# Second-to-last block through the short residual path, a bias addition split by tiles and issued at another place, and two projections exchanged at the end of the first layer

## The chip, the cores and the metric

The kernel runs on one core of a Trainium2 chip. The time is that of one execution on the device, in microseconds (us). Before the change three runs gave 1673.42, 1675.89 and 1676.69 us; the median is 1675.89 us. Lower is better.

## What is computed

Four sub-layers follow each other on 4 x 1024 tokens of 256 numbers each. Every one is `x = x + layernorm(f(layernorm(x)))`:

```python
x = x + _layernorm(_L0_attn_ref(_layernorm(x), ...))   # gated attention in groups of 64
x = x + _layernorm(_L0_ffn_ref(_layernorm(x), ...))    # low-rank feed-forward, 256-64-1024-64-256
x = x + _layernorm(_L1_attn_ref(_layernorm(x), ...))   # 16 heads, relu scores divided by their sum
x = x + _layernorm(_L1_ffn_ref(_layernorm(x), ...))    # 8 experts, each takes its top tokens
...
def _L1_attn_ref(x, w_qkv, w_out, b_out, gamma, beta):
    ...
    out = out @ w_out + b_out
    y = x + out
    ...
```

The change is in the first two sub-layers (the "first layer") and in the hand-over to the third. `b_out` is the output's bias that the title speaks of; in the kernel it is added to the normalised input `h` ahead of time, because `h` is what `out @ w_out` is later added to.

## The kernel before

**Tiling.** The 4096 tokens are 8 blocks of 512 (`NB = 8`), each held as four tiles of 128 tokens (`NJ = 4`) by 256 numbers. A batch row is two blocks (`BPB = 2`). The residual stream `xs[0]` to `xs[7]` stays in SBUF from start to end.

**Engines.** TensorE (PE) does all matrix products and transposes. VectorE (DVE) and ScalarE (ACT) empty PSUM, make statistics and scale. GpSimd (POOL) has a few element-wise additions and the power -1/2 of each layer norm. PE, DVE and ACT execute in the order in which the kernel is written (`manual_schedule` names just these three). POOL is not among them: the tool that builds the program places POOL's instructions itself.

**The first layer** is one pipeline over the blocks. In iteration `t` of the loop, the attention of block t, the projections of block t+1, and the feed-forward of block t-1 (in part t-2) are woven together step by step on PE (`woven`, `attend`, `project`, `feed_forward`). In iteration 7 there is no block 8, and the projections of the second layer's first row stand in its place: `project_row` with steps `turn` (transpose `h`), `queries`, `keys`, `values`, for `k = 0` and `k = 1` (blocks 0 and 1).

**Side work on DVE and ACT** is written as chains (`Chain`, `start`): lists of pairs of a gap and a step. `on_pe` issues one PE step, advances a clock of planned time by the step's length, and then issues those chain steps that are due. A larger gap therefore puts a step later in the order of DVE and ACT, behind the work that other steps issue there.

**The usual path** from attention to the feed-forward of a block is `add_normalized("c", t, y)`: four statistics of `y` (`stc`, `mvc`), `vec`, the power on POOL (`rsc`, L539), `msc` (L543), four scalings of `y` on ACT (L549), one addition `x += y` of 128x1024 on POOL (L560). Then come four statistics of `x` (`stf`, `mvf`), `vef`, `rsf` on POOL, `msf`, four scalings `f` on DVE (L807), and the PE transpose of `f` (`turn` in `feed_forward`, L818) with which the feed-forward begins.

**The short path**, `ahead` in `feed_forward`, is in use for block 7 alone: the statistics of each tile of `y` are made as soon as the tile is there (`then` in `attend`); ACT subtracts the mean from `x` in four pieces (`shift_x`, L909), and DVE adds `y * rs` to `x` tile by tile (L915) and makes the statistics of that tile at once. POOL's 128x1024 addition falls away.

**The bias** `b1o` (from `b_out`) is added by POOL to all of `h` after the second `turn` of a block (L339), one instruction of 128x1024; it must stand behind the transposes, which need `h` without it. `h` is read again only when the second layer closes that block (L1128).

**The end of the first layer** (the loop over `*left[:2], ..., second["values1"], keys0, keys0`) is PE work of the last feed-forwards and of the second row's projections. The last three steps are `values1` of block 1 and then `keys0` of blocks 0 and 1. `keys` empties its PSUM through ACT (L357) and then DVE (L358) into `kT`; the scores of the second layer (L1217) need `kT`.

The gaps concerned are these:

```python
POW, ADD = 4.0, 4.0
SOON = 2.0
gap = POW if t < NB - 2 else SOON                                            # add_normalized, L562
gap, add_gap = (POW, ADD) if t < NB - 2 else (SOON, ADD - 1.0)               # feed_forward, usual path, L900
gap = SOON                                                                   # feed_forward, short path, L918
```

Of the kernel before, what the change touches and what calls it, by code (L numbers as in the profile page):

```python
# [13 lines left out]
ALU = mybir.AluOpType  # L14
# [4 lines left out]
P = 128  # L19
D = 256  # L20
DC = D // P
TB = 512
NJ = TB // P
# [48 lines left out]
def kernel(  # L72
# [32 lines left out]
    nc = tc.nc  # L105
    B, S, _ = x_in.shape
    NT = B * S
    NB = NT // TB
    NTILE = NT // P
    BPB = S // TB  # L110
# [109 lines left out]
    with ExitStack() as st1:  # L220
# [101 lines left out]
            row["v"] = act_v("vaug")  # L322
            return row

        def row_steps(row, k, bank, new_hT):

            h = row["h"][k]
            cols = slice(k * TB, (k + 1) * TB)
            d = {}

            def turn(c):
                if c == 0:
                    d["hT"] = new_hT()
                tp = bank([P, NJ, P], "tp")
                for i in range(NJ):
                    nc.tensor.transpose(tp[:, i, :], h[:, i, c * P : (c + 1) * P], ident)
                nc.scalar.copy(d["hT"][c], tp.rearrange("p j t -> p (j t)"))
                if c == DC - 1:
                    nc.gpsimd.tensor_tensor(h, h, b1o.unsqueeze(1).to_broadcast([P, NJ, D]), ALU.add)  # L339

            def rows_of(w, t, name):
                pp = bank([P, TB], name)
                for c in range(DC):
                    nc.tensor.matmul(  # L344
                        pp, lhsT=w[:, c, t * P : (t + 1) * P], rhs=d["hT"][c], start=(c == 0), stop=(c == DC - 1)
                    )
                return pp

            def queries(t):
                nc.scalar.copy(row["qT"][:, t, cols], rows_of(wq1, t, "pq"))  # L350

            def keys(t):
                if t not in row["kT"]:
                    row["kT"][t] = act8("hid", "kT").rearrange("p (r a) n -> p r (a n)", r=2)
                kT = row["kT"][t]
                pk = rows_of(wk1, t, "pk")
                nc.scalar.activation(kT[:, 0, cols], pk, AF.Copy, scale=strip[:, 0:1])  # L357
                nc.vector.tensor_scalar(kT[:, 1, cols], pk, strip[:, 1:2], None, ALU.mult)  # L358

            def values(z):  # L360
                v = row["v"]
                if (k, z) == (0, 0):
                    nc.gpsimd.memset(v[:, :, :, HD : HD + 1], 1.0)
                pv = bank([P, 2, D], "pv")
                for y in range(2):
                    i = 2 * z + y
                    for c in range(DC):
                        nc.tensor.matmul(  # L368
                            pv[:, y, :],
                            lhsT=d["hT"][c][:, i * P : (i + 1) * P],  # L370
                            rhs=wv[:, c, :],
                            start=(c == 0),
                            stop=(c == DC - 1),
                        )
                j = k * NJ + 2 * z
                nc.scalar.copy(
                    v[:, j : j + 2, :, 0:HD].rearrange("p j h d -> p (j h) d"),
                    pv.rearrange("p j (h d) -> p (j h) d", d=HD),
                )

            return {"turn": turn, "queries": queries, "keys": keys, "values": values}
# [124 lines left out]
        def start(*steps):  # L506
            chains.append(Chain(steps))
            return chains[-1]
# [10 lines left out]
                time["spent"] += 1.0  # L519

        POW, ADD = 4.0, 4.0
        SOON = 2.0

        def stats_steps(tag, src):

# [27 lines left out]
        def add_normalized(tag, t, y):  # L553

            r, stats, scales, shift = stats_steps(tag, y)

            def apply(i0):
                apply_on_act(y(), y(), r, i0)
                if i0:
                    nc.gpsimd.tensor_tensor(xs[t], xs[t], y(), ALU.add)  # L560

            gap = POW if t < NB - 2 else SOON  # L562
            return [*stats, (0.0, scales), (gap, shift), (0.5, lambda: apply(0)), (0.0, lambda: apply(2))]

        def open_block(t):
# [165 lines left out]

        def project_row(row, k, new_hT, chain):

            steps = row_steps(row, k, bank, new_hT)

            def turn(z):
                chain.finish()
                steps["turn"](z)

            named = {f"turn{z}": (0.6, lambda z=z: turn(z)) for z in range(2)}  # L740
            for name in ("queries", "keys", "values"):
                for z in range(2):
                    named[f"{name}{z}"] = (1.75, lambda name=name, z=z: steps[name](z))
            return named
# [53 lines left out]
        def feed_forward(t, y, ahead=None):  # L798

            d = {}  # L800
# [96 lines left out]
                start(*add_normalized("g", t, lambda: d["y"]))  # L897

            if ahead is None:
                gap, add_gap = (POW, ADD) if t < NB - 2 else (SOON, ADD - 1.0)  # L900
                adding = [*add_normalized("c", t, y), (add_gap, stats[0][1]), *stats[1:]]
            else:

                ra, scales_a, shift_a = ahead

                def shift_x():
                    shift_a()
                    for i in range(NJ):
                        nc.scalar.activation(  # L909
                            xs[t][:, i, :], xs[t][:, i, :], AF.Identity, bias=ra["ms"][:, i : i + 1]  # L910
                        )

                def add(i):
                    x = xs[t][:, i, :]
                    nc.vector.scalar_tensor_tensor(x, y()[:, i, :], ra["rs"][:, i : i + 1], x, ALU.mult, ALU.add)  # L915
                    stats[i][1]()

                gap = SOON  # L918
                adding = [(0.0, scales_a), (gap, shift_x), *((0.0, lambda i=i: add(i)) for i in range(NJ))]
# [30 lines left out]
        for t in range(NB):  # L950
            opening.finish()
            coming, after = after, None
            to_hidden, hidden, from_hidden = ffn
            adding = ahead = then = None
            if t == 0:
                whole = later_counts()
            elif t == 1:
                mb1, strip, same_b, earlier_b, bits, counts, fold = later_constants(whole)
                count_p, count_c, count_t, in_tile = (
                    whole[name] for name in ("count_p", "count_c", "count_t", "in_tile")  # L960
                )
            if coming is not None:
                own = project(coming)
                adding = start(*residual(coming))
            else:

                row0 = open_row(hs)
                inputs = opening, start(*normalize_row(hs[1], 1))
                of_row = [project_row(row0, k, new, inputs[k]) for k, new in enumerate((first_hT, second_hT))]
                own = [  # L970
                    of_row[0][name]
                    for name in ("turn0", "turn1", "queries0", "queries1", "keys1", "values0", "values1")
                ]
                d["y"] = wk.tile([P, NJ, D], F32, tag="nT", name="y", bufs=1)
                ra, stats, scales_a, shift_a = stats_steps("c", lambda d=d: d["y"])
                ahead, then = (ra, scales_a, shift_a), lambda i, stats=stats: stats[i][1]()
            if t + 2 < NB:
                after, steps = open_block(t + 2)
                opening = start(*steps)
            elif coming is not None:  # L980

                d["y"] = act4("y")
                hs = [act4("h") for _ in range(BPB)]
                opening = start(*normalize_row(hs[0], 0))
            beside = woven(left, own, to_hidden)
            main = attend(d, then)
            while main:
                on_pe(*main.pop(0))
                if not beside and hidden:
                    on_pe(*hidden.pop(0))  # L990
                places = max(len(main) - len(hidden), 0) + 1
                for _ in range(-(-len(beside) // places)):
                    on_pe(*beside.pop(0))
            for step in (*beside, *hidden):
                on_pe(*step)
            if adding is not None:
                adding.finish()
            left = from_hidden
            ffn = feed_forward(t, lambda d=d: d["y"], ahead)
            chains.insert(0, chains.pop())  # L1000
            d = coming
# [3 lines left out]
        for step in (  # L1005
# [6 lines left out]
            *to_hidden[2:],  # L1012
            *hidden,
            *from_hidden,
            second["values1"],
            *(of_row[k]["keys0"] for k in range(BPB)),
        ):
            on_pe(*step)
        for chain in chains:
# [7 lines left out]
    with ExitStack() as st3:  # L1027
# [243 lines left out]
                    rest[:0] = divide(state, t)  # L1271

        row = row0
        before = None
        for b in range(B):
            after = open_row() if b + 1 < B else None
# [397 lines left out]
```

## Time and profile before

| what | us |
| --- | --- |
| median of three runs (lowest, highest) | 1675.89 (1673.42, 1676.69) |
| the profiled execution, its own time | 1674.0 |
| its span, first to last instruction | 1671.5 |
| PE busy in the span | 1548.5 (93%) |
| DVE, ACT, POOL busy | 914.9, 634.6, 388.1 |
| first layer, from the start to about | 428 |
| PE busy in the stretch 310 to 432 | 111.3 of 122 |
| PE busy in the second layer's attention, 432 to 1090 | 653.0 of 658 |

The profile is of one execution. Its times run from the first instruction, and 2.5 us of the execution's 1674.0 us lie outside of the span. A line of the timeline gives the start and the length in us, the engine, the source line, the operation, the tiles written and read, the shape, and how many instructions are merged in it; in brackets stands how long the engine sat idle before, and what released it. PE matmuls of float32 appear as two records each.

### The profile page before, as it was taken

How to read it: one execution, taken by the hardware profiler on the slowest of the kernel's cores; microseconds unless marked ns; L12 is line 12 of the kernel's file. 1: busy time of each engine (PE TensorE's matmuls, PEld its weight loads, DVE VectorE, ACT ScalarE, POOL GpSimd, SP SyncE). 2: the span in 40 equal slices, each digit the busy share in tenths (PEclk: the TensorE clock that was granted, in tenths of full speed). 3: DMA queues.
4: the chain of work that ended last, by engine and by line, in shares of the span. 5: the costliest groups of instructions: out<-in, count | busy, mean ns of one | idle time of the engine just before them, and what ended most of it. 6: DMA issues, size and time to landing. Idle time of an engine off the chain costs nothing.

```text
span 1671.5 us, 22249 instructions
## 1 busy us (share of the span) xinstructions
PE 1548.5 (93%) x8663; PEld 770.4 (46%) x8663; DVE 914.9 (55%) x2046; ACT 634.6 (38%) x1099; POOL 388.1 (23%) x396
## 2 busy tenths in 40 slices
PE   7999999998999999999999999924999999999990
PEld 3666666665222232323222222202765766667670
DVE  4555556654657787878787888775121122212115
ACT  3344444534444545454545455421212122121213
POOL 4122233222201010201011101012332432433325
PEclk9999999999999999999999999955999999999995
DMA  8300000000000000000000000041233333423217
GB/s 210 107 1 1 1 1 1 1 1 1 1 1 1 14 14 13 15 13 14 14 14 1 13 5 10 8 147 26 63 66 76 68 67 71 93 46 84 32 19 208
DMA packets 66195, 64.31 MB, mean 38 GB/s; under 512 B 23181, under 2 KB 60074, under 8 KB 65962
## 3 DMA queue, kind: packets, MB, share of 16 engines
q1 hardware_dynamic: 52352, 42.81, 8.5%
q0 software_dynamic: 12864, 19.14, 6.9%
q8 instruction: 68, 1.11, 0.3%
q10 hardware_dynamic: 874, 0.93, 0.2%
q14 instruction: 37, 0.30, 0.1%
HBM read 39.64 MB, written 23.23 MB: 38 GB/s over the span
## 4 chain that ended last, share of the span: by engine, by line
PE 91%; DVE 3%; issue 3%; POOL 1%; DMA 1%; ACT 1%; SPq 0%; POOLq 0%; ACTq 0%; DVEq 0%
PE sc L1217 16%; PE po L1233 15%; PE py L1548 13%; PE ph L1526 13%; PE pg L679 3%; PE py L787 3%; PE pv L695 3%; PE pv L368 2%; PE ph L843 2%; PE po L759 2%; PE pt L1121 2%; PE pk L344 2%; PE pq L344 2%; PE pq L864 2%; PE po L763 1%
## 5 line engine op out<-in xcount | busy, mean ns | idle before, releaser
L1227 DVE TENSOR_SCALAR w<-sc 128x1024 f32<-128x1024 f32 x256 | 312.6, 1222 | 97.1 <-PE sc L1217 64.1
L1226 ACT ACTIVATE w<-sc 128x512 f32<-128x512 f32 x512 | 278.0, 594 | 229.1 <-PE sc L1217 102.5
L1217 PE MATMUL sc<-qT,kT 32*128 32x512 f32 x2048 | 293.6, 639 | 2.3 <-DVE kT L358 1.6
L1233 PE MATMUL po<-w,vaug 128*17 128x512 f32 x2048 | 274.7, 598 | 0.9 <-DVE w L1227 0.2
L1548 PE MATMUL py<-w,hid 128*128 128x256 f32 x1024 | 230.1, 380 | 0.0
L1533 ACT ACTIVATE hid<-ph,mb 128x512 f32<-128x512 f32 (+1 forms) x136 | 90.1, 662 | 365.4 <-PE ph L1526 365.4
L1526 PE MATMUL ph<-xT,w 128*128 128x512 f32 (+1 forms) x544 | 224.7, 572 | 0.5 <-DVE xT L1510 0.4
L1548 PEld LDWEIGHTS py<-w,hid 128*128 128x128 f32 x1024 | 191.1, 190 | 32.0 <-issue 7.5
L1217 PEld LDWEIGHTS sc<-qT,kT 32*128 32x128 f32 x2048 | 80.8, 183 | 186.1 <-issue 170.7
L1526 PEld LDWEIGHTS ph<-xT,w 128*128 128x128 f32 x544 | 104.6, 193 | 111.6 <-issue 107.6
L1562 POOL DMA_INDIRECT acc_d<-y,idx x64 | 101.3, 1582 | 211.5 <-issue 150.7
L1233 PEld LDWEIGHTS po<-w,vaug 128*17 128x17 f32 x2048 | 35.3, 95 | 200.0 <-issue 171.0
L1560 DVE TENSOR_TENSOR y<-py,mb 128x256 f32<-128x256 f32 x64 | 26.8, 418 | 183.9 <-PE py L1548 183.9
L1485 POOL DMA_INDIRECT got<-tok_d,idx x64 | 66.0, 1031 | 152.9 <-DVE idx L1481 135.8
L1510 DVE COPY xT<-tp 128x512 f32<-128x512 f32 (+1 forms) x34 | 22.4, 660 | 97.4 <-PE tp L1508 97.4
L1053 POOL TENSOR_TENSOR rsg<-veg,mhalf 128x1 f32<-128x1 f32 x32 | 17.8, 555 | 219.2 <-DVE veg L1052 219.2
L679 PE MATMUL pg<-nT,wh 128*128 128x512 f32 x128 | 61.6, 613 | 1.5 <-ACT nT L618 1.5
L787 PE MATMUL py<-wo,oT 128*128 128x256 f32 x256 | 61.9, 385 | 0.0
L695 PE MATMUL pv<-wh,nT 128*128 128x512 f32 x128 | 59.7, 593 | 0.0
L1481 DVE CAST idx<-parts 128x8 int32<-128x8 f32 x8 | 1.3, 167 | 101.9 <-PE parts L1479 101.9
L787 PEld LDWEIGHTS py<-wo,oT 128*128 128x128 f32 x256 | 47.3, 190 | 17.2 <-issue 9.4
L560 POOL TENSOR_TENSOR x<-x,y 128x1024 f32<-128x1024 f32 x15 | 35.3, 2353 | 75.7 <-ACT y L549 75.7
(262 smaller groups left out, 1855.0 us busy)
## 6 DMA issues: line engine op xcount, KB each, us to landing
w<-in_L_ffn_W_dram SPq DMA_DIRECT2D x16, 1024.0 KB, 5.7
x<-in_L_attn_x_dram SPq DMA_DIRECT2D x8, 512.0 KB, 5.0
acc_d<-logits SPq DMA_DIRECT2D x8, 512.0 KB, 5.1
tok_d<-hg SPq DMA_DIRECT2D x32, 128.0 KB, 1.8
back<-acc_d SPq DMA_DIRECT2D x7, 512.0 KB, 9.2
out_dram<-x SPq DMA_DIRECT2D x16, 128.0 KB, 1.7
out_dram<-back POOLq DMA_DIRECT2D x4, 512.0 KB, 6.7
out_dram<-x SPq DMA_DIRECT2D x3, 512.0 KB, 3.4
```

The costliest lines, as they stand in the source:

```text
L344: nc.tensor.matmul(pp, lhsT=w[:, c, t * P : (t + 1) * P], rhs=d["hT"][c], start=(c == 0), stop=(c == DC - 1))
L679: nc.tensor.matmul(pg, lhsT=wh[:, c, HID + e * P : HID + (e + 1) * P], rhs=d["nT"][:, c, :], start=(c == 0), stop=(c == DC - 1),)
L695: nc.tensor.matmul(pv, lhsT=d["nT"][:, c, i * P : (i + 1) * P], rhs=wh[:, c, 0:HID], start=(c == 0), stop=(c == DC - 1),)
L787: nc.tensor.matmul(py, lhsT=d["oT"][:, e, :], rhs=wo[:, e, :], start=(e == 0), stop=(e == EC - 1))
L1217: nc.tensor.matmul(sc, lhsT=row["kT"][t][rows, r, kt * P : (kt + 1) * P], rhs=row["qT"][rows, t, qh * TB : (qh + 1) * TB], start=True, sto ...
L1226: nc.scalar.activation(w[:, j, :], sc, AF.Relu)
L1227: nc.vector.tensor_scalar(w[:, 2:4, :], pair, 0.0, None, ALU.max)
L1233: nc.tensor.matmul(po[32 * j : 32 * j + HD + 1, :], lhsT=row["v"][:, kt, HQ * t + 2 * j + r, :], rhs=w[:, j, :], start=(kt == 0), stop=(kt ...
L1526: nc.tensor.matmul(ph, lhsT=w1[:, c, f * P : (f + 1) * P], rhs=xT[u][:, c, h * n : (h + 1) * n], start=(c == 0), stop=(c == DC - 1),)
L1533: nc.scalar.activation(hid[:, f, h * n : (h + 1) * n], ph, AF.Gelu, bias=mb1[:, e * FC + f : e * FC + f + 1])
L1548: nc.tensor.matmul(py, lhsT=hid[:, f, i * P : (i + 1) * P], rhs=w2[:, f, :], start=(f == 0), stop=(f == FC - 1),)
L1562: scatter = nc.gpsimd.indirect_dma_start(out=acc_d[:, :], out_offset=bass.IndirectOffsetOnAxis(ap=lists[e].idx[:, k : k + 1], axis=0), in_ ...
```

## The change

Five edits:

- Block 6, the second to last, takes the short path too. The lines that set `ahead` and `then` move from the branch of iteration 7 to a place that iterations 6 and 7 both reach.
- The gaps: `SOON` becomes 1.0. With that the short path of both blocks plans 1.0 behind each power. In `add_normalized` the gap is 4.0 for all blocks but the last, which keeps 2.0; so block 6's second normalisation (tag "g", after its feed-forward) goes from 2.0 to 4.0.
- The bias is added by four instructions of 128x256 in place of one of 128x1024, in both layers (`add_bias`).
- For the first row (`row0`, blocks 0 and 1) the bias is not added in `turn` but by two calls of `add_bias` at the start of the second layer's main loop.
- At the end of the first layer both `keys0` come ahead of `values1`.

```diff
+        def add_bias(row, k):
+
+            for i in range(NJ):
+                nc.gpsimd.tensor_tensor(row["h"][k][:, i, :], row["h"][k][:, i, :], b1o, ALU.add)
+
-        def row_steps(row, k, bank, new_hT):
+        def row_steps(row, k, bank, new_hT, with_bias=True):
...
-                if c == DC - 1:
-                    nc.gpsimd.tensor_tensor(h, h, b1o.unsqueeze(1).to_broadcast([P, NJ, D]), ALU.add)
+                if c == DC - 1 and with_bias:
+                    add_bias(row, k)
...
-        SOON = 2.0
+        SOON = 1.0
...
-            gap = POW if t < NB - 2 else SOON
+            gap = POW if t < NB - 1 else 2.0
...
-            steps = row_steps(row, k, bank, new_hT)
+            steps = row_steps(row, k, bank, new_hT, False)
...
-                gap, add_gap = (POW, ADD) if t < NB - 2 else (SOON, ADD - 1.0)
-                adding = [*add_normalized("c", t, y), (add_gap, stats[0][1]), *stats[1:]]
+                gap = POW
+                adding = [*add_normalized("c", t, y), (ADD, stats[0][1]), *stats[1:]]
...
-                ra, stats, scales_a, shift_a = stats_steps("c", lambda d=d: d["y"])
-                ahead, then = (ra, scales_a, shift_a), lambda i, stats=stats: stats[i][1]()
...
+            if t >= NB - 2:
+                ra, stats, scales_a, shift_a = stats_steps("c", lambda d=d: d["y"])
+                ahead, then = (ra, scales_a, shift_a), lambda i, stats=stats: stats[i][1]()
...
-            second["values1"],
             *(of_row[k]["keys0"] for k in range(BPB)),
+            second["values1"],
...
         row = row0
+        for k in range(BPB):
+            add_bias(row, k)
```

## The prediction

> **What bounds the kernel now.** I read the page, PE's waits up to 432 us, and then the timeline of the end of the first layer engine by engine. The page gives the bound:
>
> ```profile
> span 1671.5 us, 22249 instructions
> ...
> PE 1548.5 (93%) x8663; PEld 770.4 (46%) x8663; DVE 914.9 (55%) x2046; ACT 634.6 (38%) x1099; POOL 388.1 (23%) x396
> ...
> PE 91%; DVE 3%; issue 3%; POOL 1%; DMA 1%; ACT 1%; SPq 0%; POOLq 0%; ACTq 0%; DVEq 0%
> ```
>
> PE is the chain. Faster side work gains only where PE waits for it. PE's waits between 362 and 432 us (waiting line, releaser: total, times, longest):
>
> ```profile
> PE tp L818 <- DVE f L807: 6.5, 2, 3.3
> PE sc L1217 <- DVE kT L358: 1.6, 1, 1.6
> PE sc L1217 <- ACT w L1226: 0.7, 1, 0.7
> ```
>
> In the second layer's main part PE is busy 653.0 of 658 us: nothing to win there, something to lose. PE's timeline places the waits:
>
> ```profile
> 361.54 1.88 PE L344 MATMUL pk<-hT,wk 128*128 128x512 f32 x4
> ...
> 367.42 1.36 PE L818 MATMUL tp<-ident,f 128*128 128x128 f32 x4 [3.15 <-DVE f L807]
> 368.57 3.21 PE L368 MATMUL pv<-wv,hT 128*128 128x256 f32 x8
> ...
> 375.57 1.89 PE L368 MATMUL pv<-wv,hT 128*128 128x256 f32 x8
> ...
> 404.04 1.83 PE L818 MATMUL tp<-ident,f 128*128 128x128 f32 x8 [3.33 <-DVE f L807]
> 405.67 3.43 PE L368 MATMUL pv<-wv,hT 128*128 128x256 f32 x8
> ...
> 428.10 1.98 PE L1217 MATMUL sc<-qT,kT 32*128 32x512 f32 x10 [1.56 <-DVE kT L358]
> 430.81 1.14 PE L1217 MATMUL sc<-qT,kT 32*128 32x512 f32 x6 [0.74 <-ACT w L1226]
> ```
>
> Wait A (3.15 us) is for block 6's `f`, wait B (3.33) for block 7's. The eight `pv` matmuls behind each take 3.05 and 3.36 us from start to next start, those at 375.57 only 1.73. The windows (PE, PEld, DVE, ACT, POOL busy; then PE's clock) say why:
>
> ```profile
> 367.40:371.60 4.20, 4.18 (x12) 3.18 (x13) 1.86 (x7) 0.59 (x1) 0.00 (x0) 0.59 0.00 0
> 371.60:375.60 4.00, 4.00 (x30) 3.73 (x29) 1.92 (x7) 1.17 (x2) 0.00 (x0) 1.00 0.00 0
> ...
> 404.00:409.00 5.00, 4.96 (x16) 3.52 (x16) 2.04 (x8) 1.16 (x2) 1.01 (x1) 0.66 0.01 3
> ```
>
> After each wait the clock is down. So the waits cost more than their length. POOL and DVE inside them:
>
> ```profile
> 353.57 2.36 POOL L339 TENSOR_TENSOR h<-h,b1o 128x1024 f32<-128x1024 f32 x1 [1.38 <-PE tp L336]
> ...
> 393.93 2.36 POOL L339 TENSOR_TENSOR h<-h,b1o 128x1024 f32<-128x1024 f32 x1 [3.33 <-PE tp L336]
> ```
>
> ```profile
> 353.60 2.35 DVE L543 SCALAR_TENSOR_TENSOR msc<-mvc,rsc 128x4 f32<-128x4 f32 x1
> ...
> 394.47 2.10 DVE L915 SCALAR_TENSOR_TENSOR x<-y,rsc,x 128x256 f32<-128x256 f32 x1 [1.11 <-ACT x L909]
> ...
> 397.17 0.45 DVE L915 SCALAR_TENSOR_TENSOR x<-y,rsc,x 128x256 f32<-128x256 f32 x1
> ```
>
> The same `x` addition takes 0.45 us alone and 2.10 us while POOL adds the bias; a 128x4 `msc` (0.15 elsewhere) takes 2.35.
>
> **What the Trainium skill says.** "TensorE: Matmul & The Clock Gate", What's actually happening: about 3.4 us of idling halves PE's clock, about 3.4 us of work restores it. The trace agrees roughly: 0.59 and 0.66 follow waits of 3.15 and 3.33 us, while after the 1.56 us wait at 428 the clock stays 1.00. "SBUF — State Buffer", Who interferes with whom: a DVE instruction with two SBUF inputs and a GpSimd one that reads SBUF exclude each other for a whole instruction, and the one that issues first goes first. The 2.10 above agrees. "GPSIMD Engine Reference", 3.1 Elementwise: an addition costs 2.6 cycles of 1.2 GHz per element, 2.22 us for 1024; the trace has 2.36.
>
> **Part 1: block 6 by the short path (wait A).** The changed program's order leaves PE's alone but for the end. DVE's and ACT's change.
> Before: `y`'s last tile is written at 345.4; the four `stc` stand behind `oT` at 348.67; `vec` 350.92; `rsc` to 352.19; `msc` held to 355.95 by the bias; ACT scales to 358.05; POOL adds to 360.49; `stf` to 363.2; then DVE sits behind a `kT` until 364.84; `rsf` 365.08 to 366.18; `f` 366.87; PE 367.42.
> After: one `stc` per tile beside the attention (0.55 us each, where DVE waits 1.5 to 2.7 us for PE); `vec` behind the same `oT`, 348.7; `rsc` 1.02 us to 350.0; `msc` 350.2; ACT, idle there, shifts (4 in 1.70) to 352.0; DVE adds from 350.75. One L915 with its statistics takes 1.05 (the spacing 397.17 to 398.21); four of them, `qT` 0.34 and `kv` 0.6 end at 355.9, with two or three waits for the split bias at about 357; `vef`, `rsf` 1.2; `f` in two halves around the two `y2` writes (1.25), done at 361. PE comes for it at 364.27, 3 us later. `kT` now stands behind `f`. So wait A goes whole: 3.15. Its cold clock goes too: `tp` plus `pv` took 4.20 us (367.42 to 371.62), warm 0.43 (the four at 326.70) + 1.73 = 2.16; 2.04. **A: -5.2.** Next late would be the PSUM bank of the second `pq` (359.82 on PE): the first `y2` write now ends at about 359.7, where it ended at 358.0. Up to 0.5 could come back.
>
> **Part 2: the bias and block 7 (wait B).** In the changed program's order POOL has the four additions exactly where the one was: behind `rsc`, ahead of `rsf`, for both blocks. POOL's order isn't the kernel's, so "later" does not come about. They still start when the transposes end, beside block 7's L915. What changes is the length: by the page's price 256 elements are an estimated 0.55 us, plus 0.14 that the long one has over its price: 0.7. From both sides: an L915 waits for nothing, or for all four (2.8). I take one tile at most each time: at 218.68 to 221.5 DVE and POOL passed the port to and fro, two DVE `head` in 1.58 and two POOL ones in 1.99, neither waiting for both.
> On the clock of before: `msc` still sits behind `qT` (393.3); ACT now shifts ahead of both `hT`, so x tile 0 is ready at 393.9, not 394.35; L915 waits to 394.2 for tile 0 of the bias; four rounds of 1.05 plus some 0.6 of further waits: 398.9; `y2` writes 1.2; `vef`, `rsf` 1.3; `f` 401.6 (before 403.49; a `kT` of 0.65 in that stretch moves behind `f`); PE 402.1, before 404.04. PE itself comes later by 0.4, as `hT` 0 waits behind the shifts (its first `pq` at 395.65 for 394.84; `hT` 1 is where it was). Wait B thus shrinks from 3.33 to about 1.0, and its end by 2.1 (bounds: 0.2 if all four tiles win, 2.9 without any waiting). At 1 us no cold clock: `tp` and `pv` took 4.99, warm 2.60, of which 0.5 is PE running behind the four `f` anyway; 1.9. **B: -4.0** (0 to -4.8).
>
> **Part 3: gaps and keys first (end).** Block 6's second scaling moves on ACT behind all eight `hid`: the last `hid` no longer waits 1.96 us, `pq` (L864) takes 3.6 for 4.09: -0.45. But it ends at 418.95, POOL's `x` addition at 421.35, and the `y2` buffer that block 7 writes is free only then: 0.6 later than PE delivers (420.67). From there `y2` to `msg` (statistics, power) ends at 427.0, with ACT's `vaug` before it done at 426.65. `keys0` first makes `kT` ready at 426.4 under `values1`, and the scores start at 426.75, not 428.10, now waiting for `vaug`'s copy. Still they run only two groups: the third PSUM buffer needs the first ACT `w`, which stands behind the four L549 (2.07): 427.1 + 2.07 + 0.6 = 429.75, before 430.81. **End: -1.05** (0 if the buffer wait is longer, -2.3 if neither wait stays).
>
> **Part 4: bias tiles in the second layer.** Six rows, four tiles for one: 2.8 for 2.37 us of POOL, nothing on PE as long as DVE isn't waiting for the `rsb` behind it. Cost 0.
>
> **Sum.** 5.2 + 4.0 + 1.05 = 10.2 us, on the profiled 1674.0: 1663.8. The median of before is 1.9 above that execution; against it 1665.7. The parts' bounds give 4.7 to 12.3, so 1663.6 to 1671.2, and single runs of before spread over 3.3.
>
> **Rivals.**
> - *The port stays shut.* The four tiles follow each other without a gap, block 7's first L915 waits for all, B keeps 2.8 us and the cold clock. For: POOL's queue is full at that moment, DVE's is not. Against: 218.68. -5.2, -0.4, -1.05: 1669.2.
> - *The wait moves.* DVE, loaded with four L915 and `stf` between 350 and 357, frees PSUM banks late, and PE stops at `pq` or `po` in place of `tp`. For: the `pq` margin of 0.1. Against: `po`'s is 0.5 and the next ones over 1. It would have to eat 7 us of A and B: about 1673.
> - *Slower.* In the second layer `rsb` stands behind the bias on POOL, DVE waits in order for `rsb`, `w` (L1227) behind it, and PE two groups later. If a tile costs 1.1 us (a 128x4 power takes 1.02) the bias is 4.4, 2.0 longer, in each of six rows. It decides from 10.2 / 6 = 1.7 us a row. At 2.0, with nothing of it hidden, it is +12 - 10.2: 1677.7. Against: PE waits nowhere in those rows now though a bias of 2.37 already stands there.
>
> **How the numbers follow.** Forecast 0.67, port 0.17, moved wait 0.09, slower 0.07. The likeliest: 1665.7. The range 1661.5 to 1671.5 is the parts' bounds with the runs' spread on the low side; it holds the port too. What a measurement can tell from no change is 0.2%, 3.4 us, so faster is below 1672.5: 0.67 + 0.17 + a third of the moved wait = 0.87; same 0.06; slower 0.07.
>
> **What would show it.** A: no PE idle before L818 near 364, clock 1.00 behind it. B: the wait near 397 (5.2 earlier) of 0.5 to 1.5 us, no cold `pv`, and POOL's four 128x256 of about 0.7 with L915 of at most 1.1. End: scores released by `vaug`, a second wait on `w`. Wrong if B is over 2.5 us with a clock of 0.66, if PE waits in the second layer behind a bias, or if the bias is found elsewhere on POOL.

## The result and the profile after

Four runs of the changed kernel take 1663.58 us in the median (1663.14 to 1663.88); the kernel before takes 1676.29 beside them (four runs). The ratio is 0.9928, with a 95% interval of 0.9910 to 0.9945. The profiled executions are 10.45 us apart: 1674.0 before, 1663.55 after. In the changed file a line stands 5 to 8 further down; L823 is the old L818, L812 the old L807, L920 the old L915, L349 the old L344, L554 the old L549, L1223 the old L1217, L1232 the old L1226. The bias is L328. The kernels of e1 and e10 to e12 have line numbers of their own. Matmuls at a lowered clock are called cold here, at the full clock warm.

The page of the changed kernel, the same three lines as before:

```profile
span 1661.6 us, 22279 instructions
...
PE 1544.9 (93%) x8663; PEld 769.6 (46%) x8663; DVE 913.8 (55%) x2050; ACT 634.0 (38%) x1099; POOL 390.5 (23%) x419
...
PE 90%; issue 3%; DVE 3%; POOL 2%; DMA 1%; ACT 1%; SPq 0%; POOLq 0%; ACTq 0%; DVEq 0%
```

POOL has 23 more instructions and 2.4 us more work, PE the same number of matmuls and 3.6 us less busy time, most of it because matmuls that ran cold at the end of the first layer no longer do. PE's waits in the last part of the first layer (waiting line, releaser: total, times, longest):

```profile
PE tp L823 <- DVE f L812: 0.9, 1, 0.9
PE sc L1223 <- ACT w L1232: 0.8, 1, 0.8
PE pq L349 <- ACT hT L342: 0.7, 1, 0.7
PE sc L1223 <- ACT vaug L381: 0.7, 1, 0.7
...
```

The lines left out are three waits of 0.5 to 0.6 at `ph` and `py`, which the kernel before has too. The 6.5 us for `f` are down to 0.9, and the wait for `kT` is gone. PE's timeline at the three places:

```profile
362.69 0.60 PE L823 MATMUL tp<-ident,f 128*128 128x128 f32 x4
363.13 1.89 PE L373 MATMUL pv<-wv,hT 128*128 128x256 f32 x8
...
395.19 1.64 PE L823 MATMUL tp<-ident,f 128*128 128x128 f32 x8 [0.91 <-DVE f L812]
396.67 1.89 PE L373 MATMUL pv<-wv,hT 128*128 128x256 f32 x8
...
416.25 1.98 PE L1223 MATMUL sc<-qT,kT 32*128 32x512 f32 x10 [0.67 <-ACT vaug L381]
419.01 1.13 PE L1223 MATMUL sc<-qT,kT 32*128 32x512 f32 x6 [0.78 <-ACT w L1232]
```

At block 6's `tp` there is no bracket any more, and both `pv` groups take 1.89 us where they took 3.21 and 3.43. The windows behind both places (PE, PEld, DVE, ACT, POOL busy; then PE's clock) have the clock at 1.00, where it was 0.59 and 0.66:

```profile
362.69:366.59 3.90, 3.90 (x22) 3.44 (x21) 3.71 (x11) 1.21 (x3) 0.00 (x0) 1.00 0.00 0
395.19:398.50 3.31, 3.31 (x17) 2.34 (x17) 3.21 (x11) 1.07 (x2) 0.00 (x0) 1.00 0.02 5
```

What POOL and DVE do ahead of block 7's `f`:

```profile
386.85 3.15 POOL L328 TENSOR_TENSOR h<-h,b1o 128x256 f32<-128x256 f32 x4 [3.00 <-PE tp L341]
```

```profile
387.18 0.67 DVE L920 SCALAR_TENSOR_TENSOR x<-y,rsc,x 128x256 f32<-128x256 f32 x1 [0.58 <-ACT x L914]
...
388.45 0.95 DVE L920 SCALAR_TENSOR_TENSOR x<-y,rsc,x 128x256 f32<-128x256 f32 x1
...
390.00 0.45 DVE L920 SCALAR_TENSOR_TENSOR x<-y,rsc,x 128x256 f32<-128x256 f32 x1
```

POOL's four tiles lie where the one instruction lay, behind the transposes of `h`: issuing them at a later place of the program moved nothing, as the prediction said. Two of DVE's additions stretch, to 0.67 and 0.95 for 0.45; none is held for 2.1.

For the experiments the trace is cut at starts of PE steps that every kernel has. A runs from the `pkv` at 340.79 (after: 339.38) to the `py` behind block 6's `pv` (371.62; 364.86). B runs from there to block 7's `pp` (409.03; 398.50). The end runs to the second group of scores (430.81; 419.01). "To tpg" runs from that first `pkv` through nearly all of the second layer's attention, to the `tpg` at 1078.31 (1066.89). All times are in us.

| kernel | A | B | end | to tpg | median (runs) |
| --- | --- | --- | --- | --- | --- |
| before | 30.83 | 37.41 | 21.78 | 737.52 | 1676.29 (4) |
| changed | 25.48 | 33.64 | 20.51 | 727.51 | 1663.58 (4) |
| changed, second profile (e9) | 25.48 | 33.64 | 20.51 | 727.51 | 1662.93 (5) |
| e1: short path alone | 26.58 | 37.97 | 21.82 | 736.92 | 1669.34 (20) |
| e3: bias of row 0 in one piece | 25.48 | 35.08 | 20.51 | 728.96 | 1663.75 (4) |
| e8: short path's gap 2.0 | 25.82 | 36.34 | 20.51 | 730.57 | 1666.44 (5) |
| e4: bias in the second layer | 25.48 | 32.93 | 20.52 | 728.81 | 1664.74 (4) |
| e10: bias behind `f` | 25.48 | 32.93 | 20.52 | 726.79 | 1662.72 (5) |
| e2: values first | 25.48 | 33.63 | 21.37 | 731.44 | 1664.69 (5) |
| e5: scaling's gap 2.0 | 25.48 | 33.63 | 20.63 | 727.60 | 1663.65 (5) |
| e13: both taken back | 25.48 | 33.63 | 21.79 | 728.73 | 1666.59 (5) |
| e14: before, keys first | 30.40 | 37.38 | 20.64 | 735.91 | 1672.67 (21) |

The changed kernel's stages are shorter by 5.35, 3.77 and 1.27 us, together 10.39; to `tpg` it is 10.01, so the second layer gives 0.38 back. Two executions of it give the same four numbers; what differs between them lies outside of these stretches (e9, below). The kernel before is less steady, as its A and B contain a cold stretch each, and that isn't always equally long: A is the same program in e14 and takes 30.40 for 30.83, B in e1 and takes 37.97 for 37.41. So the gains in A and B are known to about half a us.

The kernel before beside the experiments had medians of 1673.80 (24 runs, with e1, e3, e4, e8), 1675.62 (9, with e2, e5, e9, e10), 1673.44 (9, with e11 to e13) and 1673.27 (25, with e14).

### The profile page after: what moved, and what is told of

It reads as the page before. It is cut to its first block, busy times and chain, and to the rows that moved or that the text cites. A ratio compares the mean times of both kernels' runs of the same rounds, so it can differ in the third digit from the quotient of the medians.

```text
span 1661.6 us, 22279 instructions
## 1 busy us (share of the span) xinstructions
PE 1544.9 (93%) x8663; PEld 769.6 (46%) x8663; DVE 913.8 (55%) x2050; ACT 634.0 (38%) x1099; POOL 390.5 (23%) x419
## 3 DMA queue, kind: packets, MB, share of 16 engines
q8 instruction: 68, 1.11, 0.3%
## 4 chain that ended last, share of the span: by engine, by line
PE 90%; issue 3%; DVE 3%; POOL 2%; DMA 1%; ACT 1%; SPq 0%; POOLq 0%; ACTq 0%; DVEq 0%
PE sc L1223 16%; PE po L1239 15%; PE py L1556 13%; PE ph L1534 13%; PE py L792 3%; PE pg L684 3%; PE pv L700 3%; PE pt L1127 2%; PE ph L848 2%; PE po L764 2%; PE pv L373 2%; PE pq L349 2%; PE pq L869 2%; PE po L768 2%; PE pk L349 1%
## 5 line engine op out<-in xcount | busy, mean ns | idle before, releaser
L1232 ACT ACTIVATE w<-sc 128x512 f32<-128x512 f32 x512 | 277.9, 595 | 229.7 <-PE sc L1223 102.6
L1223 PE MATMUL sc<-qT,kT 32*128 32x512 f32 x2048 | 293.6, 640 | 1.5 <-ACT w L1232 0.8
L1223 PEld LDWEIGHTS sc<-qT,kT 32*128 32x128 f32 x2048 | 80.8, 183 | 184.9 <-issue 170.7
```

Source lines behind the costliest of these rows:

```text
L1223: nc.tensor.matmul(sc, lhsT=row["kT"][t][rows, r, kt * P : (kt + 1) * P], rhs=row["qT"][rows, t, qh * TB : (qh + 1) * TB], start=True, sto ...
L1232: nc.scalar.activation(w[:, j, :], sc, AF.Relu)
```

## The experiments

### e1: the short path alone

```diff
-                ra, stats, scales_a, shift_a = stats_steps("c", lambda d=d: d["y"])
-                ahead, then = (ra, scales_a, shift_a), lambda i, stats=stats: stats[i][1]()
...
+            if t >= NB - 2:
+                ra, stats, scales_a, shift_a = stats_steps("c", lambda d=d: d["y"])
+                ahead, then = (ra, scales_a, shift_a), lambda i, stats=stats: stats[i][1]()
```

> The kernel before with one part of the change: block 6 goes by the short path (statistics of y beside the attention, shift on ACT, four L915-type additions on DVE). The gaps, the bias as one 128x1024 addition behind the last transpose, and values1 ahead of keys0 stay as they were before. Theory (the wait of block 6 and the cold clock behind it are the short path's alone): no PE wait over 0.5 us at block 6's tp, clock 1.00 behind it, the stretch up to block 7 5.0 to 5.5 us shorter; the wait at block 7's tp stays at 2.8 to 3.4 us with its cold pv, the end stays. In all about 5.3 us less than before, 1669 to 1671. Rival (the wait only moves): PE stops at pq or po by 1 us or more in that stretch, in all 0 to 3 us. Second rival (the split bias is what frees block 6): the one long bias holds L915 of block 6 for over 2 us and a wait of 1 us or more is left at tp.

PE's timeline of this kernel at block 6, then DVE's, then PE's at the first scores:

```profile
360.69 1.98 PE L344 MATMUL pq<-hT,wq 128*128 128x512 f32 x4 [0.47 <-DVE y L891]
362.51 1.88 PE L344 MATMUL pk<-hT,wk 128*128 128x512 f32 x4
...
365.09 0.60 PE L818 MATMUL tp<-ident,f 128*128 128x128 f32 x4
365.52 1.89 PE L368 MATMUL pv<-wv,hT 128*128 128x256 f32 x8
```

```profile
354.20 1.88 DVE L915 SCALAR_TENSOR_TENSOR x<-y,rsc,x 128x256 f32<-128x256 f32 x1
```

```profile
424.33 2.35 PE L1218 MATMUL sc<-qT,kT 32*128 32x512 f32 x10 [1.56 <-DVE kT L358]
427.04 2.08 PE L1218 MATMUL sc<-qT,kT 32*128 32x512 f32 x6 [0.37 <-ACT w L1227]
429.06 1.91 PE L1234 MATMUL po<-w,vaug 128*17 128x512 f32 x8
```

The wait for block 6's `f` is gone and its `pv` is warm: A is 4.25 us shorter, by the short path alone. That is less than the expected 5.0 to 5.5 and 1.10 short of the whole 5.35. The one long bias holds the second L915 for 1.88 us, and the `y2` writes then free PE's bank late: PE waits at the second `pq`, the spot that the prediction named as next (0.47 in brackets; it starts 1.0 us later behind A's `pkv` than in the changed kernel). The table says what removes this: with the tiles and the old gap (e8) 0.34 of the 1.10 is left, with the gap of 1.0 and the bias in one piece (e3) nothing. There DVE has three of the four additions behind it when the bias starts. So the tiles help block 6, but the smaller gap alone is enough. B keeps its 3.3 us wait. This execution then loses 2.7 us more at the scores, where PE runs cold from within the first ten `sc` on: the six `sc` take 2.08 us where they took 1.14 before. Its own time, 1673.05, is one of six runs at 1672.1 to 1674.1; the other fourteen lie at 1668.6 to 1670.1.

### e3 and e8: what shortens the wait at block 7

e3 puts row 0's bias back into one instruction each, at the same place:

```diff
         for k in range(BPB):
-            add_bias(row, k)
+            h0 = row["h"][k]
+            nc.gpsimd.tensor_tensor(h0, h0, b1o.unsqueeze(1).to_broadcast([P, NJ, D]), ALU.add)
```

> The changed kernel, but the bias of row 0's two halves is one 128x1024 addition each instead of four 128x256, issued at the same place of the program; the second layer keeps its tiles. Theory (the tiles let DVE's x additions in between POOL's): block 7's first L920 is held about 2.1 us in place of 0.67, PE's wait at block 7's tp is 2.2 to 2.7 us in place of 0.91; the tp and pv behind it run at the low clock if a wait of that length brings it (then 3 to 3.5 us slower than the changed kernel, without it 1.3 to 1.8). Rival (tiles are worth nothing, the smaller gap and the order of ACT's shifts do it all): within 0.5 us of the changed kernel.

e8 keeps the tiles and puts the gap back:

```diff
-        SOON = 1.0
+        SOON = 2.0
```

> The changed kernel, but with the gap of the short path at 2.0 as it was, not 1.0: on ACT block 7's four shifts stand behind the first hT and not ahead of both; DVE's msc of block 6 stands behind three statistics and qT. Theory: the first pq of row 0's second half no longer waits 0.71 us for hT, but x tile 0 comes 0.4 to 0.5 later, so block 7's f comes 0.3 to 0.6 later; in PE's time the end of the wait at block 7's tp moves by +0.3 to +0.6, in all that much slower; block 6 stays without a wait. Rival (the gap is worth more, as the first L920 would then come behind all of the bias tiles): 1.5 us or more slower. Rival (no worth): within 0.2 us.

e3, DVE and then PE:

```profile
387.13 2.62 DVE L920 SCALAR_TENSOR_TENSOR x<-y,rsc,x 128x256 f32<-128x256 f32 x1 [0.58 <-ACT x L914]
```

```profile
396.59 1.64 PE L823 MATMUL tp<-ident,f 128*128 128x128 f32 x8 [2.36 <-DVE f L812]
398.07 1.89 PE L373 MATMUL pv<-wv,hT 128*128 128x256 f32 x8
```

e8, DVE and then PE:

```profile
395.72 0.42 DVE L537 BATCH_NORM_STATS2 stg<-y 128x6 f32<-128x256 f32 x1
...
396.80 0.72 DVE L363 TENSOR_SCALAR kT<-pk,strip 128x512 f32<-128x512 f32 x1
397.43 0.15 DVE L548 SCALAR_TENSOR_TENSOR msf<-mvf,rsf 128x4 f32<-128x4 f32 x1
397.50 1.38 DVE L812 TENSOR_SCALAR f<-x,mvf,rsf 128x256 f32<-128x256 f32 x4
```

```profile
398.06 2.21 PE L823 MATMUL tp<-ident,f 128*128 128x128 f32 x8 [2.55 <-DVE f L812]
400.06 2.76 PE L373 MATMUL pv<-wv,hT 128*128 128x256 f32 x8
```

Without the tiles the first L920 waits out the whole bias (2.62 us), and PE's wait is 2.36: the tiles are worth 1.44 us in B. The `pv` behind it is still warm. With the gap at 2.0 the wait is 2.55, this time with a cold `tp` and `pv` behind it, and B is 2.70 longer, far more than the expected 0.3 to 0.6: `tp` starts 1.32 later, and the cold stretch costs 1.38 more. Of the 1.32, ACT's shift is 0.53: DVE sat idle 1.11 us for it ahead of the first L920, not 0.58. About 0.5 is the order that the lines above show: statistics of `y2` and a `kT` now stand between `vef` and `f`. The statistics cost nothing, since they end at 396.88 and `rsf` is done only at 396.91, but the `kT` behind them runs to 397.5, and `f` starts at 397.50, 0.59 behind `rsf` instead of 0.11. With the gap at 1.0 both stand behind `f`. The rest is small (the first L920 takes 0.82 for 0.67, and the `y2` writes stand ahead of the fourth). In its run times e3 (1663.24 to 1665.10) can't be told from the changed kernel, whose first profile loses 1.7 us at a cold `pt` in the second layer that e3's does not lose (e9).

### e4 and e10: the bias really later

In e4 the tiles read a copy of the bias that DVE makes at the start of the second layer, so that POOL can't start earlier:

```diff
+        b1l = wk.tile([P, D], F32, tag="b1l", name="b1l", bufs=1)
+        nc.vector.tensor_copy(b1l, b1o)
         for k in range(BPB):
-            add_bias(row, k)
+            for i in range(NJ):
+                h0 = row["h"][k][:, i, :]
+                nc.gpsimd.tensor_tensor(h0, h0, b1l, ALU.add)
```

> The changed kernel, but the bias of row 0 is added really later: the four tiles of each half read a copy of the bias that is made at the start of the second layer, so that POOL adds them there and not beside block 7. Theory (what is left of the wait at block 7's tp is the last of the bias): all four L920 take 0.45 us, the wait of 0.91 falls to 0.1 to 0.4, in all 0.5 to 0.9 us less than the changed kernel, nothing lost in the second layer. Rival (the rest of the wait is DVE's own chain): the wait stays over 0.7. Rival (the place in the second layer costs): a new PE wait there of 0.5 us or more.

DVE and PE of e4 at the scores:

```profile
420.39 0.29 DVE L1281 COPY b1l<-b1o 128x256 f32<-128x256 f32 x1 [4.04 <-POOL x L565]
420.60 1.22 DVE L1233 TENSOR_SCALAR w<-sc 128x1024 f32<-128x1024 f32 x1
```

```profile
421.87 1.04 PE L1239 MATMUL po<-w,vaug 128*17 128x512 f32 x4 [1.31 <-DVE w L1233]
```

At block 7 it does what was expected: all L920 take 0.45 to 0.48 us, the wait at `tp` is 0.21, B is 0.71 shorter. The price comes later, and it is the copy's: the copy waits 4.04 us for POOL's last `x` addition, and DVE's `w` stands behind the copy. (Its tile probably lies in memory that this addition still uses; the trace shows only the wait.) PE's next scores come 4.38 us behind the second group, where they come 2.05 behind it in the changed kernel, and to `tpg` e4 is 1.30 us longer.

e10 holds back only the second half's tiles, with DVE copying one column of `h` onto itself behind `f`:

```diff
+        def touch():
+            h1 = row0["h"][1][:, :, 0:1]
+            nc.vector.tensor_copy(h1, h1)
...
             *to_hidden[:2],
+            (0.0, touch),
             second["values0"],
```

> The changed kernel, but the bias of row 0's second half is held back until block 7's f is written: DVE copies one column of each tile of h onto itself (128x4, about 0.15 us) behind f, and the four POOL tiles have to wait for it; no tile and no copy in the second layer. Theory (as e4_bias_late showed at block 7, without its price in the second layer, which was the copy that waited 4.04 us for POOL and held DVE's w): all four L920 take 0.45 to 0.48 us, the wait at tp falls from 0.91 to 0.1 to 0.3, and the 0.7 us stays won to the end of the first layer and in the second: 0.6 to 0.9 us less than the changed kernel where the clock is alike. Rival (the bias behind f delays rsg on POOL and with it the y2 chain): the gain is given back at the scores, within 0.2 us.

POOL of e10:

```profile
392.66 1.01 POOL L544 TENSOR_TENSOR rsf<-vef,mhalf 128x4 f32<-128x4 f32 x1 [8.97 <-DVE vef L542]
397.62 2.77 POOL L328 TENSOR_TENSOR h<-h,b1o 128x256 f32<-128x256 f32 x4 [3.95 <-DVE h L1013]
400.36 1.01 POOL L544 TENSOR_TENSOR rsg<-veg,mhalf 128x4 f32<-128x4 f32 x1
```

The bias is behind `f`, the wait at `tp` is 0.20, and the 0.71 us stays: to `tpg` it takes 726.79 us where the changed kernel takes 727.51. `rsg` comes later, but nothing on PE waits for it. In the runs the gain can't be seen: 1661.15 to 1663.19, beside 1662.33 to 1663.62 for the changed kernel.

### e2, e5 and e13: the end

e2 takes the order back, e5 the gap of block 6's second scaling, e13 both:

```diff
-            *(of_row[k]["keys0"] for k in range(BPB)),
             second["values1"],
+            *(of_row[k]["keys0"] for k in range(BPB)),
```

```diff
-            gap = POW if t < NB - 1 else 2.0
+            gap = POW if t < NB - 2 else 2.0
```

> The changed kernel with the second half's values1 ahead of both keys0 at the end of the first layer, as before. Theory (keys first takes the kT off the end of the chain): the first scores wait for DVE's kT again, 1.4 to 1.6 us in place of 0.67 for vaug, the second wait on ACT's w stays at 0.7 to 0.8; the end 0.8 to 1.0 us later. Rival (the end hangs on y2's second statistics and on ACT's four L554, whichever comes first on PE): within 0.2 us. A kT wait of this length may also drop the clock in some executions, which would add 1 to 2.7 us to those.

> The changed kernel with the gap of block 6's second scaling at 2.0 again, so that ACT's four L554 of block 6 stand between the hid and not behind all of them. Theory: pq (L869) takes 4.1 in place of 3.67 us (+0.45), as the last hid waits for the scaling; but POOL's x addition is done before PE's py, so the y2 additions do not wait 1.70 (0.6 beyond PE), and the chain to the scores is about as long: in all 0 to +0.5 us. Rival (the larger gap behind hid is a gain by itself): +0.5 to +1.0. Rival (the buffer wait weighs more): 0.2 to 0.6 faster.

> The changed kernel with both edits of the end taken back: values1 ahead of keys0, and the gap of block 6's second scaling at 2.0. Taken back one at a time they cost 0.77 and 0.11 us up to the second scores, while the changed kernel stands 1.27 better there than the one before. Theory (they overlap: with keys first the end hangs on ACT's w behind L554, which the smaller gap pulls forward again, while with kT last PE's own queue sets the end and the 0.42 us of pq is lost whole): the second scores come 1.2 to 1.3 us later than in the changed kernel, relative to block 7's pp. Rival (the two add): 0.9. A drop of the clock at the kT wait can add 1 to 3 us in some executions.

PE of e2, e5 and e13, in this order:

```profile
417.06 1.98 PE L1223 MATMUL sc<-qT,kT 32*128 32x512 f32 x10 [1.56 <-DVE kT L363]
419.78 2.08 PE L1223 MATMUL sc<-qT,kT 32*128 32x512 f32 x6 [0.74 <-ACT w L1232]
```

```profile
417.45 1.98 PE L1223 MATMUL sc<-qT,kT 32*128 32x512 f32 x10 [0.68 <-ACT vaug L381]
419.90 1.13 PE L1223 MATMUL sc<-qT,kT 32*128 32x512 f32 x6 [0.47 <-ACT w L1232]
```

```profile
418.46 1.98 PE L1223 MATMUL sc<-qT,kT 32*128 32x512 f32 x10 [1.56 <-DVE kT L363]
421.18 1.13 PE L1223 MATMUL sc<-qT,kT 32*128 32x512 f32 x6 [0.74 <-ACT w L1232]
```

Taken back alone, the order costs 0.86 us and the gap 0.12; together 1.28, all of the end's gain. They overlap: put into the kernel before alone, keys first brings 1.14 (e14, below). With keys first the second scores hang on ACT's `w`, and with the old gap the `w` wait is only 0.47, which pays back most of the 0.42 us that `pq` loses. With values first PE's queue up to `kT` sets the end, and `pq` counts whole. In e2's profiled execution PE ran cold again, though not directly behind the 1.56 us wait: the ten `sc` there take 1.98, as in e13, and only the six behind the next wait, of 0.74, take 2.08 for 1.13. It took 1667.07 us, the other four 1664.35 to 1665.24.

### e9 and e14: why the runs scatter

e9 is the changed kernel unaltered.

> The changed kernel once more, unaltered, to see how far TensorE's clock alone moves its time. Theory (two places are decided by where the clock's drop falls: the first pg matmuls after the start, 2.6 to 3.8 us for the same four, and the pt matmuls behind the 2.29 us wait at the end of the second layer, 3.3 or 5.0 us): the waits of the first layer's end are as in the first profile within 0.1 us each, while pg and pt may differ by 1.1 and 1.7; runs between 1661 and 1665. Rival (both are properties of the program): pg again 2.6 to 2.8 and pt again 5.0.

The first matmuls and those behind the one long wait at the end of the second layer's attention, in the first profile of the changed kernel:

```profile
12.23 2.68 PE L684 MATMUL pg<-nT,wh 128*128 128x512 f32 x4
...
1071.45 4.97 PE L1127 MATMUL pt<-wop,oT 128*128 128x256 f32 x14 [2.29 <-DVE oT L1112]
```

and in e9:

```profile
12.22 3.78 PE L684 MATMUL pg<-nT,wh 128*128 128x512 f32 x4
...
1072.80 3.29 PE L1127 MATMUL pt<-wop,oT 128*128 128x256 f32 x14 [2.29 <-DVE oT L1112]
```

The same program, the same waits: the four `pg` differ by 1.10 us and the `pt` by 1.68, in opposite directions here. What these two places cost is luck, then, and no property of the program. All fourteen traces of this study have the 2.29 us wait; `pt` was cold behind it in seven and warm in seven.

e14 is the kernel before with keys first, made because in e1 and e2 the clock dropped near the `kT` wait:

```diff
-            second["values1"],
             *(of_row[k]["keys0"] for k in range(BPB)),
+            second["values1"],
```

> The kernel before with one edit: both keys0 ahead of values1. Theory (the 1.56 us wait for kT is what drops the clock in some executions of the kernel before, whose 42 runs so far lie in two groups, 27 at 1672.1 to 1674.4 us with a mean clock of 0.965 to 0.968 and 15 at 1675.2 to 1676.9 with 0.964): from block 7's pp to the second scores 20.6 us in place of 21.8, about 1.15 less, and in the runs no second group 2.5 us above the first: all of them between 1671 and 1673.5. Rival (the groups come from elsewhere, the two waits for f or the start): about 1.15 less, but still two groups.

The stage is as expected, 20.64 us (-1.14). The theory on the groups falls: the 21 runs still lie in two, eleven at 1670.35 to 1672.67 and ten at 1673.75 to 1675.70. Since nearly half of them are in the upper one, the medians hardly differ (ratio 0.9998, 0.9991 to 1.0005), although the stretch is 1.1 us shorter. Two such groups showed in the three kernels that keep the 3.3 us wait at block 7 (before, e1, e14). The nine runs of the changed kernel, which lost that wait, lie within 1.6 us, but the four of e4, which has no such wait either, spread over 3.0. Which place makes the groups stays open: there is one profile of each of those kernels, so none from both groups of the same one.

### e11 and e12: further

e11 adds to e10 that block 7's last scaling runs behind the first scores of the second layer, in ACT's idle time, with `y2` in a tile that is free by then. e12 adds that `keys0` of the first half fills PE's wait for `qT`.

```diff
+                if t == NB - 1:
+                    d["y"] = d["hid"][1].rearrange("p a (b n) -> p (a b) n", n=D)[:, :NJ, :]
...
+        late = chains.pop()
         for chain in chains:
             chain.finish()
+        while len(late.steps) > 4:
+            late.go()
...
+        rest.extend(do for _, do in late.steps)
```

```diff
-            *from_hidden,
-            *(of_row[k]["keys0"] for k in range(BPB)),
+            *from_hidden[:2],
+            of_row[0]["keys0"],
+            *from_hidden[2:],
+            of_row[1]["keys0"],
             second["values1"],
```

> The kernel with the bias behind f, and block 7's last scaling (power, msg, four L554, POOL's x addition) moved behind the first scores of the second layer, one step for each group; its y2 lies in block 7's second hid, which down2 has read, so that it no longer waits for POOL. Theory (the 0.78 us wait of the second scores is ACT's w standing behind the four L554, and ACT has 0.97 us idle in each group of the second layer): that wait goes, y2's 1.70 us wait becomes about 1.1 (PE's py), 0.6 to 0.8 us less than the kernel with the bias behind f. Rival (the scaling holds w in the groups where it now stands): waits of PE on w in the first five groups of the second layer of the same length, within 0.2 us.

> The kernel with the last scaling moved into the second layer, and keys0 of row 0's first half put between down2 and up2 of block 7. Theory (PE's 0.53 us wait for qT is filled with matmuls that are due anyway, and y2 no longer stands ahead of the scores): the wait for qT goes, 0.4 to 0.6 us less than without this. Rival (y2's statistics, now later on DVE, stand ahead of w and hold the scores): the gain comes back as a wait on DVE's w, within 0.2 us.

PE and ACT of e12:

```profile
415.38 2.94 PE L1236 MATMUL sc<-qT,kT 32*128 32x512 f32 x16 [0.68 <-DVE stg L537]
418.25 1.05 PE L1252 MATMUL po<-w,vaug 128*17 128x512 f32 x8
```

```profile
418.84 1.08 ACT L554 ACTIVATE hid<-hid,msg,rsg 128x256 f32<-128x256 f32 x2
420.46 1.09 ACT L1245 ACTIVATE w<-sc 128x512 f32<-128x512 f32 x2 [0.54 <-PE sc L1236]
```

All sixteen `sc` run without a stop, and the scaling lies between ACT's `w`. From `pp` to the first `po` group it is 21.57 us in the changed kernel, 21.59 in e10, 20.63 in e11 and 20.23 in e12. To `tpg` e11 takes 725.75 and e12 725.01: 1.76 and 2.50 less than the changed kernel, 0.72 of it from the bias behind `f` as in e10, and 0.33 in e12 because a wait for `turned` is missing there ("Second layer", below). The medians, 1662.73 and 1662.90, don't show it; e12's runs go from 1658.55 to 1663.27, and in its profile `pt` was cold (4.81). Against the kernel before the ratio of e12 is 0.9926 (0.9913 to 0.9940), that of the changed kernel in e9 0.9929 (0.9916 to 0.9943). So e12 is shorter up to `tpg`, but not shown to be a faster kernel.

## Why the prediction was right, and where it was off

**A** was put at -5.2 and measured at -5.35. The wait (3.15) and the cold clock behind it went as worked out; `f` of block 6 was done at 358.9, 3.8 us ahead of PE. The size agrees better than it had to: with e14's A as the measure it would be -4.9. The "next late" bank of the second `pq` didn't bite in the changed kernel, but in e1 it did, and the smaller gap is what keeps it from biting.

**B** was put at -4.0 and measured at -3.77. Block 7's `tp` comes 2.09 us earlier behind A's end, the wait is 0.91 (said: about 1.0), and the `tp` and `pv` behind it take 3.31 us where they took 4.99, so 1.68 (said: 1.9). The sum used 2.1 for the wait's end, but its own working gives 404.04 - 402.1 = 1.94; that the 2.1 came out is luck. The pieces were named rightly: L915 held for about a tile at a time (0.67 and 0.95), ACT's shift earlier by 0.45 (0.53), the `kT` moved behind `f` (about 0.5). What the prediction missed is that the pieces need each other. Counted from the kernel before, `tp` comes 0.64 us earlier with the small gap alone (e3), 0.77 with the tiles alone (e8) and 2.09 with both. Beside one long bias the earlier shift only makes DVE wait longer, 2.62 for 2.10. So "What changes is the length" is half of the reason: taken out of the changed kernel, the gap costs 2.70 us in B, 1.38 of it cold clock, and the tiles 1.44.

**The port rival** was priced at 1669.2 with the wait at 2.8 and a cold clock. e3 comes near to it: the addition is held 2.62, the wait is 2.36, but `pv` stays warm. So the bias in one piece would have cost 1.4 us, not 3.6; a wait of 2.55 did bring the cold clock in e8, so this may come out otherwise in another execution. The Trainium skill, "SBUF — State Buffer", Who interferes with whom, calls the port pair that DVE and GpSimd share an exclusive lock and has the order of issue decide who blocks. The traces agree: 2.62 us beside one POOL instruction of 2.35, 0.67 and 0.95 beside four short ones.

**The end** was put at -1.05 and measured at -1.27. The path was named rightly: `vaug`, then ACT's `w`, releases the scores, and the `y2` writes did wait for POOL's addition:

```profile
410.73 1.29 DVE L896 TENSOR_TENSOR y<-py,b 128x512 f32<-128x512 f32 x2 [1.70 <-POOL x L565]
```

The working followed one path with both edits in it, which was right, as they don't add: 0.86 and 0.12 taken back alone, 1.28 together.

**Second layer**, put at 0: 0.38 us is lost, 0.33 of it in one wait of `po` for `turned` at 1020. e1, whose bias is in one piece there, loses 0.40 with the same 0.33 us wait, so it isn't the tiles. What moved that wait stays open. PE's only other wait there, 0.2 for `w`, is in the kernel before too, so nothing speaks for the "slower" rival.

**The median.** Against its own execution the sum gave 1663.8, and the profiled execution of the changed kernel took 1663.55. That they are so close is partly luck: in the changed kernel's profile A begins 1.41 us earlier, 1.10 of it at the first `pg`, and the `pt` behind `tpg` takes 1.68 more, and the two nearly cancel. The prediction then added the 1.9 us by which the median of before stood above its profile, and came to 1665.7. That term failed, and it makes up nearly all of the 2.1 us by which the likeliest value missed: the changed kernel's median lies 0.03 above its profiled execution. The runs of before lie in two groups and those of the changed kernel don't, so the offset wasn't a constant to be carried over; what makes the groups is open (e14). Even so, a difference of medians is the worse measure here: it is 12.7 us in both comparisons in which the two kernels ran side by side, and would be 10.3 to 10.9 with the other medians of before against e9's 1662.93, while the program is 10.0 shorter up to `tpg`.

## What to carry to other kernels

A planned gap between a side chain's steps is also a decision on what other work stands ahead of the next step on an engine that executes in order: when it changes, list what ends up ahead of the last instruction that the bound engine waits for. When two engines exclude each other instruction by instruction, cutting the one's long instruction lets the other in: here that brought 1.44 of the 2.15 us that taking it out of the way altogether brings (e3 against e10). Two edits to the same chain can need each other, so try each from both sides, added to the kernel before and taken out of the changed one. Where the clock of the bound engine depends on its waits, compare kernels by stretches of the trace that contain no such place, or say how much such a place scatters: whole times carried 1 to 3 us of luck here, while the tiles were worth 1.44 us in B, keys first 0.86 and the gap of the second scaling 0.12.

## What was not expected of the hardware

- The clock can drop behind waits shorter than those of before, and not always: behind single waits of 0.91 and 0.2 us never, 2.29 us in seven of fourteen traces, 2.36 not (e3), 2.55 yes (e8), 3.15 and 3.33 in all five cases. At the first scores, where a wait of 1.56 us and one of 0.4 to 0.7 stand about 2 us apart, it dropped in e1 and e2 but not in e13 or before, in e1 already among the ten `sc` between the two waits, in e2 only behind the second. The Trainium skill, "TensorE: Matmul & The Clock Gate", What's actually happening, lets the clock fall after an idle window of about 3.4 us that runs freely, so that where a change falls depends on where in the window the work lands. That fits the two profiles of one program (`pt` 3.29 and 4.97). The length doesn't fit: none of these waits reaches 3.4 us, and 2.29 was enough half of the time.
- In these few cases a cold stretch at the scores cost more than one at `tp` and `pv`: 3.1 us in e2 and 2.7 in e1, against 2.0 and 1.7 in the kernel before.
- Four POOL additions of 128x256 take 2.77 us with no two-input DVE addition beside them (e10) and 3.15 where DVE's additions cut in; one of 128x1024 takes 2.35. Each of the three cuts thus costs about 0.14 us.
